# Graph kernel: 60 instead of 72 slotted source buckets in the last two layers, seven instead of five fetched row tiles, and later transposes

## The chip, the cores and the metric

The kernel runs on one core of one Trainium2 chip. The metric is the device time of one execution in microseconds; the time before is the median of three runs. The core's engines are named as in the profile: PE multiplies matrices (PEld is its loading of the stationary operand), DVE, ACT and POOL compute elementwise, SP and others issue DMAs. POOL also issues the indirect DMAs that fetch rows by a list of row numbers.

## The reference, cut to what matters

A graph of N = 12500 nodes with 128 float32 features and 200000 random directed edges passes four layers in a row. Each layer sums, for every node, the rows of its neighbours (plus edge information), and sends the sum through small dense products.

```python
def gnn0(h):                                   # layer 0, messages src -> dst, then a GRU cell
    msg = h[src] @ W_msg.T + b_msg + edge_embed[edge_type]
    messages = segment_sum(msg, dst, 12500)
    return gru_cell(messages, h)               # gates of 3 x 128

def gin(x, p, concat):                         # layers 1 to 3, with self loops added to the edges
    ee = ea @ enc_w + enc_b
    h = concatenate([x[ei[1]], ee], 1) if concat else x[ei[1]] + ee
    agg = segment_sum(h, ei[0], 12500)
    h = relu(batchnorm(agg @ w1 + b1))
    return h @ w2 + b2

x = layernorm(x + gnn0(x))
h = relu(gin(x, p0, False)); h = relu(gin(h, p1, True)); h = gin(h, p2, True)
out = layernorm(x + h)
```

## The kernel before

Nodes lie in NB = 98 blocks of 128. The edges are sorted on the chip, in a preparation of about 1180 us, by the block of the node that gets the sum (the target block, `o` in the code) and by the block of the node that is read (the source bucket, `b`). Every pair of target block and bucket has SL = 32 slots; four buckets make one tile of 128 slots. Features are held as three bf16 pieces side by side (H3 = 384 columns, 768 bytes a row), so that a product with a matrix of zeros and ones selects float32 rows.

One layer walks over the 98 target blocks. For a block it does the following:

- DVE builds two matrices of zeros and ones: `g` (L1546), which says which source row fills each slot, and `s` (`st` in the code, L1551, in four pieces), which says to which node of the block each slot is added.
- For each tile PE makes four gather matmuls of 32 columns (L1663), one for each bucket, from the source tables `X` in SBUF, tiles of seven buckets (XC = 7, 672 KB), into PSUM. Up to TG = 3 tiles form a group with three PSUM banks; the pool `psg` holds two groups.
- ACT, in layers 0 and 1 with DVE's help (L1669, L1670, L1672), copies the group to SBUF as `e` (the eviction; four buffers).
- PE adds the tiles of `e` to their nodes with one scatter matmul each (L1592, in `scatter`), into one accumulating PSUM bank `acc`, of which there is only one. `add_up_to(2)`, called after every second group, does the scatters of groups that were gathered two or more groups ago.
- After a block's last group `finish` adds the three pieces of `acc` to `s` (the float32 sums; L1614, L1617, L1618 on DVE), and, after every second block, appends a dense generator to `work`: `gru` in layer 0, `gin` in layers 1 to 3. A generator runs in pieces between its `yield`s; `tick` advances the oldest one by one piece. Two ticks, or three if more than one is waiting, follow each `add_up_to`. The dense pieces are transposes of the sums (L1464 in `gin`; L1412 and L1413 in `gru`), a copy of them on DVE (`sT`, L1466), the first products (L1473, L1474; in `gru` L1427 to L1429), the activations and gates on ACT (L1476), the second products (L1484), and what writes the result into the next layer's table.

Layers 0 and 1 have all 98 buckets in slots: 25 tiles, nine groups. Layers 2 and 3 have only IC = 72 buckets in slots, 18 tiles in six groups; the edges of the other buckets are listed for each target block, and their source rows are fetched one by one: `fetch` (L1568) is an indirect DMA on POOL's queue that brings 128 rows, 98 KB, from the table in HBM to a place of a ring. `rt` = 5 such row tiles stand for each target block (980 fetches in the two layers), and a matmul for each, with the same kind of one-hot columns, adds it to the same bank (L1597, in `scatter_row`). A block's groups 1 to 5 each ask for one fetch and scatter one row tile. The ring has 14 − 11 = 3 tiles of seven places, 21; 15 fetches are issued ahead of the loop. A fetch waits for its place: for the scatter matmul that read it last. `Slots.rows` prepares the row numbers and columns of the fetched tiles in layer 0, one window for each row tile.

POOL also fetches edge attributes (L719) in layers 0 and 1, paced by small copies called `token` (L1688); in layers 2 and 3 the ring's fetches are its work. In the layers only POOL's order is written by hand; a scheduler places PE's, DVE's and ACT's instructions. Before layers 1, 2 and 3 a loop over spilled edges (L663) brings all engines together, and the source tables of the new layer are loaded by SP and ACT queues.

Of the kernel before, what the change touches and what calls it, by code (L numbers as in the profile page):

```python
# [32 lines left out]
TG = 3  # L33
# [5 lines left out]
class Plan:  # L39
    def __init__(self, lst, ic, rt):  # L40
# [3 lines left out]
        self.row = self.kept = 0  # L44
        self.width = CELL + self.cells + (CELL + self.cells) % 2


IC = 72
CELL = 5
PLANS = (Plan("C", IC, 5),)  # L50
RT = sum(p.rt for p in PLANS)
TW = CELL + NTL
assert PLANS[0].rt <= CELL and CELL % 2 == NTL % 2 == 1
OV = 8
# [34 lines left out]
def gnn_kernel(ctx: ExitStack, tc: tile.TileContext, x, xx, src, dst, ea, et, w_msg, w_ihT, w_hhT, b_msg,  # L89
# [276 lines left out]
    XC = 7  # L366
# [834 lines left out]
    with by_hand(EN.Activation, EN.PE):  # L1201
# [34 lines left out]
        n = 0  # L1236
# [156 lines left out]
    def gru(i, b0, s):  # L1393
        q = b0 // 2
        if q % 2 == 0:
            four["xx"] = dq.tile([P, 2, 2, 2 * H], F32, name="xx")
            m = min(2, NB // 2 - q)
            nc.sync.dma_start(four["xx"][:, :m], xx[:, q:q + m])
        xb = four["xx"][:, q % 2, 0, :].rearrange("p (b f) -> p b f", b=2)
        xt = four["xx"][:, q % 2, 1, :]  # L1400
        yield
        c6 = dq.tile([P, 2, 6, NTX], BF16, name="c6")
        v = s[:, :, H:]
        times = lambda n: v[:, :, None, :].to_broadcast([P, 2, n, NTX])
        V.tensor_copy(c6[:, :, 0:3, :], times(3))
        V.tensor_sub(v, v, c6[:, :, 0, :])
        V.tensor_copy(c6[:, :, 3:5, :], times(2))
        V.tensor_sub(c6[:, :, 5, :], v, c6[:, :, 3, :])
        yield
        pt = psd.tile([P, 512], F32, name="d")  # L1410
        for k in range(2):
            T.transpose(pt[:, k * P:(k + 1) * P], s[:, k, 0:H], ident)  # L1412
            T.transpose(pt[:6 * NTX, 256:384].bitcast(BF16)[:, k * P:(k + 1) * P],  # L1413
                        c6[:, k, :, :].rearrange("p a b -> p (a b)"), identb)
        sT = dq.tile([P, 2 * P], F32, name="sT")
        V.tensor_copy(sT, pt[:, :256])
        cT = dq.tile([E6, 4 * P], BF16, name="cT")[:6 * NTX, :2 * P]
        A.copy(cT, pt[:6 * NTX, 256:384].bitcast(BF16))
        yield
        yield  # L1420
        yield
        gates = dq.tile([P, 2, 2 * H], F32, name="gates")
        n = dq.tile([P, 4, H], F32, name="n")[:, 0:2, :]
        for k in range(2):
            ks = slice(k * P, (k + 1) * P)
            pg = psd.tile([P, 512], F32, name="d")
            T.matmul(pg, cT[:, ks], w["ew"], start=True, stop=False, skip_group_check=True)  # L1427
            T.matmul(pg[:, 0:3 * H], sT[:, ks], w["wa"], start=False, stop=False, skip_group_check=True)
            T.matmul(pg[:, H:], xt[:, ks], w["whh"], start=False, stop=True, skip_group_check=True)  # L1429
            A.activation(gates[:, k, :], pg[:, H:3 * H], AF.Sigmoid)  # L1430
            V.tensor_mul(n[:, k, :], gates[:, k, 0:H], pg[:, 3 * H:])
            V.tensor_add(n[:, k, :], n[:, k, :], pg[:, 0:H])
            yield
            yield
            yield
        A.activation(n, n, AF.Tanh)
        yield
        y, k, whole = rows_of(b0)
        d = dq.tile([P, 2, H], F32, name="r3")
        V.tensor_sub(d, xb, n)  # L1440
        V.tensor_mul(d, d, gates[:, :, H:])
        V.tensor_add(n, n, xb)
        V.tensor_add(y[:, k:k + 2, :], n, d)
        if whole:
            yield from layernorm(y, *whole, False)

    def gin(i, b0, s):
        yield
        k4 = b0 % 4
        if k4 == 0:  # L1450
            m = min(4, NB - b0)
            while len(summed) < b0 + m:
                next(attr)
            four["eT"] = dq.tile([E6, 4 * P], BF16, name="cT")
            nc.sync.dma_start(four["eT"][:, :m * P], eaTd[:, b0 * P:(b0 + m) * P])
            if i == 3:
                four["xx"] = dq.tile([P, 2, 2, 2 * H], F32, name="xx")
                nc.sync.dma_start(four["xx"][:, 0].rearrange("p a (b f) -> p (a b) f", b=2)[:, :m, :], x1d[:, b0:b0 + m, :])
            else:
                four["o"] = dq.tile([P, 4, H], F32, name="n")  # L1460
        eT = four["eT"][:, k4 * P:(k4 + 2) * P]
        pt = psd.tile([P, 512], F32, name="d")
        for k in range(2):
            T.transpose(pt[:, k * P:(k + 1) * P], s[:, k, 0:H], ident)  # L1464
        sT = dq.tile([P, 2 * P], F32, name="sT")
        V.tensor_copy(sT, pt[:, :256])  # L1466
        yield
        yield
        ph = psd.tile([P, 2, 2 * P], F32, name="d")
        h1 = dq.tile([P, 2, 2 * P], F32, name="gates")  # L1470
        for m in range(2):
            ms = slice(m * P, (m + 1) * P)
            T.matmul(ph[:, m, :], w["w1"][:, ms], sT, start=True, stop=False)  # L1473
            T.matmul(ph[:, m, :], w[f"wc_{i - 1}"][:, ms], eT, start=False, stop=True)  # L1474
        for m in range(2):
            A.activation(h1[:, m, :], ph[:, m, :], AF.Relu, bias=w["shift"][:, i - 1, m:m + 1],  # L1476
                         scale=w["scale"][:, i - 1, m:m + 1])
        yield
        yield
        po = psd.tile([P, 512], F32, name="d")  # L1480
        for k in range(2):
            ks = slice(k * P, (k + 1) * P)
            for m in range(2):
                T.matmul(po[:, ks], h1[:, m, ks], w["w2"][:, m, :], start=(m == 0), stop=(m == 1))  # L1484
        bias = w["b2"][:, None, :].to_broadcast([P, 2, H])
        po3 = po[:, :256].rearrange("p (b f) -> p b f", b=2)
        if i < 3:
            o = four["o"][:, k4:k4 + 2, :]
            V.tensor_add(o, po3, bias)
            yield  # L1490
            V.tensor_scalar(o, o, 0.0, None, op0=OP.max)
            split3(o, i + 1, b0, b0 + 2 == NB)
            if k4 or b0 + 2 == NB:
                nc.sync.dma_start(by_node(ovf[i + 1], b0 - k4, k4 + 2), four["o"][:, :k4 + 2, :])
        else:
            y, k, whole = rows_of(b0)
            xb = four["xx"][:, 0].rearrange("p a (b f) -> p (a b) f", b=2)[:, k4:k4 + 2, :]
            V.tensor_add(xb, xb, bias)
            V.tensor_add(y[:, k:k + 2, :], po3, xb)
            if whole:  # L1500
                yield from layernorm(y, *whole, True)
# [1 line left out]

    token = ctile([1, 1], "token", BF16)
    LATE, BEHIND = 4, 8
    assert PLANS[0].rt == -(-PLANS[0].cells // TG) - 1

    def layer(i, rate):

# [2 lines left out]
        if i < 2:  # L1512
            nb, tiles, c0, tw, cell, row, rt = NB, NTL, a * (CELL - 1), TC, a, 0, 0
        else:
            nb, tiles, c0, tw, cell, row, rt = p.ic, p.cells, 0, p.width, CELL, p.row, p.rt
        xf = -(-nb // XC)
        rb = NB // XC - xf
        wid = H3 + (NTX if cells_only else 0)
        groups = -(-tiles // TG)
        work = []  # L1520
        due = -8 if cells_only else 0
        stack = ExitStack()
# [6 lines left out]
        def slots_of(o):  # L1529

            n = nb * SL
            inr = rp.tile([P, 2 * IC * SL], BF16, name="inr")[:, :per * n]
            inr = inr.rearrange("p (b c) -> p b c", c=n)
# [38 lines left out]
        def tick():  # L1572
            if work and next(work[0], "end") == "end":
                work.pop(0)

        ready = []
        row_slots = slots.rows() if cells_only else None
        for _ in range(rb * rt):
            fetch()
        for _ in one_hots(0):  # L1580
            pass
# [1 line left out]
        picked = []  # L1583
# [8 lines left out]
                T.matmul(sums[o][:, :wid], st[:m, :, cell + t], e[:m, j, :wid], start=(t == 0),  # L1592
                         stop=(t == tiles - 1), skip_group_check=True)

        def scatter_row(o, st, j):
            if 0 <= j < rt:
                T.matmul(sums[o][:, :H3], st[:, :, row + j], place(o * rt + j), start=False, stop=False,  # L1597
                         skip_group_check=True)

# [35 lines left out]
            yield from dense  # L1635

        def add_up_to(n):
            while len(picked) > n:
                o, st, e, k = picked.pop(0)
                if k == groups - 1:  # L1640
                    scatter_row(o, st, k - 1)
                scatter(o, st, e, k)
                if k < groups - 1:
                    scatter_row(o, st, k - 1)
                if k == groups - 1:
                    finish(o)

        for o in range(NB):
            g, st = ready.pop(0)
# [5 lines left out]
            for k in range(groups):  # L1655
                n = min(TG, tiles - TG * k)
# [18 lines left out]
                    V.tensor_tensor(e[:m, :n, H3:], iota[:m, None, :NTX].to_broadcast([m, n, NTX]),  # L1675
                                    typecol[:m, o, t:t + n, None].to_broadcast([m, n, NTX]), op=OP.is_equal)
                picked.append((o, st, e, k))
                if k:
                    fetch()
                next(pieces, None)  # L1680
                if cells_only:
# [8 lines left out]
                    due -= 1  # L1690
                if (o * groups + k) % 2 == 0:
                    continue
                add_up_to(2)
                for _ in range(2 + (len(work) > 1)):
                    tick()
            for _ in pieces:
                pass
# [63 lines left out]
```

## Time and profile before

| what | value |
|---|---|
| three runs | 6322.02 us median, 6303.31 to 6328.62 |
| the profiled execution | 6326.88 us, of which the span holds 6325.1 us |
| mean granted TensorE clock | 0.884 of full speed |
| busy: PE, PEld | 4936.9 us (78%), 3045.2 us (48%) |
| busy: DVE, ACT, POOL | 3758.4 (59%), 3696.8 (58%), 3318.8 us (52%) |
| first and last gathers: layer 0, layer 1 | 1184 to 2914 us, 2915 to 4364 us |
| first and last gathers: layer 2, layer 3 | 4366 to 5338 us, 5340 to 6310 us |
| fetches of rows (L1568) | 980, 959.9 us on POOL, mean 979 ns |

The times of the layers overlap a little with what follows them: the dense work of a layer's last blocks runs while the next one begins. The page's slices of the span show this course; each digit is the share of a fortieth of the span, 158 us, in tenths:

```profile
## 2 busy tenths in 40 slices
PE   3881421378888888887888888887999998899998
PEld 3871121144444444443555454444666665566666
DVE  9976788666666666665555555553444443444444
```

The first seven slices are the preparation, the next twenty layers 0 and 1, the last thirteen layers 2 and 3. Rows of groups are read so: line, engine, operation, result and source with their shapes, the number of instructions; then busy time and the mean of one in ns; then how long the engine was idle ahead of them, and which instruction ended how much of it. In a time line a row is start, duration, engine and line, and in brackets the idle time before it with what ended it.

### The profile page before, as it was taken

To read this page: it belongs to the slowest core of one execution; us is meant where nothing else is said; L and a number is where in the kernel's file an instruction comes from. 1 tells how busy PE (TensorE), PEld (TensorE's weight loads), DVE (VectorE), ACT (ScalarE), POOL (GpSimd) and SP (SyncE) were. 2 spreads that over 40 slices of the span, in tenths; PEclk is the share of its full clock that TensorE was granted. 3 is DMA by queue.
4 is the path that set the end of the run, shared out by engine and by line. 5 is a ranking of instruction groups with operands and counts; after the bars stand their busy time and mean duration, and the time that the engine had idled before them with its cause. 6 is when DMAs were issued, how large, how long until landed. Compare 5 with 4: busy or idle time off the path is not lost. (4 is left out here: it accounts for less than half of the span.)

```text
span 6325.1 us, 129827 instructions
## 1 busy us (share of the span) xinstructions
PE 4936.9 (78%) x50669; PEld 3045.2 (48%) x50669; DVE 3758.4 (59%) x9291; ACT 3696.8 (58%) x5320; POOL 3318.8 (52%) x4247
## 2 busy tenths in 40 slices
PE   3881421378888888887888888887999998899998
PEld 3871121144444444443555454444666665566666
DVE  9976788666666666665555555553444443444444
ACT  7770211155555555554666666665777776677776
POOL 1004677366566565655666666652555553555553
PEclk9755555589999899998999999998999999999999
DMA  1001300122222222223222222223444445344443
GB/s 70 21 1 32 100 18 7 42 72 82 73 82 75 76 84 84 76 75 136 82 81 78 80 81 75 78 80 135 138 139 138 147 140 167 123 143 137 137 145 105
DMA packets 278298, 575.36 MB, mean 91 GB/s; under 512 B 74332, under 2 KB 170216, under 8 KB 277026
## 3 DMA queue, kind: packets, MB, share of 16 engines
q1 hardware_dynamic: 159138, 416.84, 19.3%
q0 software_dynamic: 105920, 116.17, 7.6%
q10 hardware_dynamic: 12616, 33.99, 1.6%
q8 instruction: 397, 6.50, 0.4%
q14 instruction: 227, 1.86, 0.1%
HBM read 478.02 MB, written 88.73 MB: 90 GB/s over the span
## 5 line engine op out<-in xcount | busy, mean ns | idle before, releaser
L1672 ACT CAST e<-g 128x1152 bf16<-128x1152 f32 (+1 forms) x2156 | 2239.6, 1063 | 844.0 <-PE g L1663 510.5
L1663 PE MATMUL g<-x,g 128*32 128x384 bf16 x33320 | 1880.7, 338 | 442.0 <-ACT e L1672 195.0
L719 POOL DMA_INDIRECT eat<-in_ea,eidcol x1666 | 1813.6, 1089 | 545.8 <-issue 416.0
L1592 PE MATMUL acc<-e,s 128*128 128x384 bf16 (+3 forms) x8428 | 1913.3, 349 | 82.3 <-DVE s L1618 53.7
L1592 PEld LDWEIGHTS <-s 128*128 128x128 bf16 (+1 forms) x8428 | 1132.0, 152 | 733.7 <-issue 515.0
L1568 POOL DMA_INDIRECT x<-table,rowcol x980 | 959.9, 979 | 955.1 <-PE acc L1597 645.2
L1663 PEld LDWEIGHTS <-g 128*32 128x32 bf16 x33320 | 807.9, 97 | 1287.2 <-issue 986.6
L1669 ACT CAST e<-g 128x768 bf16<-128x768 f32 x784 | 627.4, 800 | 574.5 <-PE g L1663 236.6
L1551 DVE TENSOR_TENSOR s<-iotas,outcol 128x832 bf16<-128x832 bf16 (+1 forms) x1568 | 875.0, 567 | 95.8 <-PE acc L1592 52.1
L1670 DVE CAST e<-g 128x384 bf16<-128x384 f32 x784 | 435.2, 555 | 576.1 <-ACT e L1669 479.0
L1688 POOL COPY token<-e 1x1 bf16<-1x1 bf16 x1412 | 344.4, 244 | 814.8 <-ACT e L1669 456.5
L1546 DVE TENSOR_SCALAR g<-inr,pidx 128x3136 bf16<-128x3136 bf16 (+1 forms) x392 | 365.0, 931 | 462.2 <-PE g L1663 439.7
L557 PE MATMUL acc<-ot,oa 125*98 125x101 bf16 x1600 | 295.9, 359 | 125.9 <-ACT ot L538 85.7
L557 PEld LDWEIGHTS <-oa 125*98 125x98 bf16 x1600 | 292.0, 277 | 129.0 <-issue 82.0
L1614 DVE TENSOR_TENSOR s<-s,acc 128x128 f32<-128x128 f32 x376 | 107.1, 285 | 414.7 <-PE acc L1592 315.5
L538 ACT ACTIVATE ot<-dbb,bias 125x160 bf16<-125x160 bf16 (+2 forms) x1078 | 332.3, 408 | 16.6 <-PE acc L557 15.9
L1597 PE MATMUL acc<-x,s 128*128 128x384 bf16 x980 | 288.5, 327 | 9.7 <-DMA x<-table,rowcol 9.7
L802 POOL IOTA num<- 98x2176 uint16 x1 | 1.9, 1946 | 459.3 <-DMA sortedB<-keyB 459.3
L1476 ACT ACTIVATE gates<-d,shift,scale 128x256 f32<-128x256 f32 x294 | 149.7, 559 | 158.6 <-PE d L1474 146.9
L752 PEld LDWEIGHTS <-eoh 128*128 128x128 bf16 x1666 | 116.7, 162 | 237.6 <-DVE eoh L746 183.3
L1675 DVE TENSOR_TENSOR e<-iota,typecol 128x30 bf16<-128x30 f32 (+1 forms) x882 | 152.9, 180 | 123.9 <-PE acc L1592 41.8
L1473 PE MATMUL d<-sT,wset 128*128 128x256 f32 x588 | 184.1, 406 | 49.3 <-DVE sT L1466 44.0
(426 smaller groups left out, 4736.5 us busy)
## 6 DMA issues: line engine op xcount, KB each, us to landing
inr<-inrow SPq DMA_DIRECT2D x196, 784.0 KB
inr<-inrow SPq DMA_DIRECT2D x98, 1152.0 KB
table<-x SPq DMA_DIRECT2D x72, 384.0 KB
eat<-in_ea,eidcol POOLq DMA_INDIRECT x1666
s<-ovf SPq DMA_DIRECT2D x69, 256.0 KB
x<-table,rowcol POOLq DMA_INDIRECT x980
x<-table ACTq DMA_DIRECT2D x19, 672.0 KB
xx<-in_xx SPq DMA_DIRECT2D x24, 512.0 KB
```

The source lines that it names most:

```text
L538: A.activation(self.ot[j % 2][:, b, :ENDS[j] - c0], dbb[:, c0:ENDS[j]], AF.Sign, bias=self.bias[:, b:b + 1], scale=-1.0)
L557: T.matmul(cps[:NB, :NB + NQ - 1], self.oa[c // HC][:, :, c % HC], self.ot[j % 2][:, :, c - (ENDS[j - 1] if j else 0)], start=(c == 0), st ...
L719: G.indirect_dma_start(out=at[:, t, :], out_offset=None, in_=ea, in_offset=bass.IndirectOffsetOnAxis(ap=eidcol[:, b, t:t + 1], axis=0))
L1546: V.tensor_scalar(g[:, :nb * SL], inr[:, o % per, :nb * SL], pidx, None, op0=OP.is_equal)
L1551: V.tensor_tensor(st[:, f0:f0 + P // 4, :], iotas[:, f0:f0 + P // 4, :tw], outcol[a][:, o, None, c0:c0 + tw].to_broadcast([P, P // 4, tw]) ...
L1568: G.indirect_dma_start(out=place(asked), out_offset=None, in_=tables[i], in_offset=bass.IndirectOffsetOnAxis(ap=rowcol[:, o, p.kept + j:p. ...
L1592: T.matmul(sums[o][:, :wid], st[:m, :, cell + t], e[:m, j, :wid], start=(t == 0), stop=(t == tiles - 1), skip_group_check=True)
L1663: T.matmul(pg[c * SL:(c + 1) * SL, j, :H3], g[:, b * SL:(b + 1) * SL], piece(X, b), start=True, stop=True)
L1669: A.copy(e[:, :2, :H3], pg[:, :2, :H3])
L1670: V.tensor_copy(e[:, 2, :H3], pg[:, 2, :H3])
L1672: A.copy(e[:m, :n, :H3], pg[:m, :n, :H3])
L1688: G.tensor_copy(token, e[0:1, 0, 0:1])
```

## The change

Four things are changed together.

The split in layers 2 and 3 is another: 60 buckets in slots instead of 72, so 15 tiles in five groups instead of 18 in six, and `rt` = 7 fetched row tiles for each target block instead of 5 (1372 fetches instead of 980). With it the source tables shrink from 11 to 9 tiles, the ring grows to 14 − 9 = 5 tiles of seven, 35 places, and 28 instead of 15 fetches are issued ahead of the loop. `g` has 1920 columns instead of 2304, and `s` 22 for each node instead of 24. `Slots.rows` does seven windows instead of five.

Row tiles are spread over all groups: `of_group(k)` gives groups 0 to 4 of a block 1, 1, 2, 1 and 2 fetches and scatters, where before each group but the first had one.

`gru` and `gin` have one empty piece more, ahead of the transposes.

`add_up_to` does one tick between `finish` of a block and the scatters of the next one, where the same call does both, and this tick is taken off those that follow.

```diff
-IC = 72
-CELL = 5
-PLANS = (Plan("C", IC, 5),)
+IC = 60
+CELL = 7
+PLANS = (Plan("C", IC, 7),)
@@ gru, behind the pieces c6 and ahead of the transposes
         yield
+        yield
         pt = psd.tile([P, 512], F32, name="d")
@@ gin, behind the loads and ahead of the transposes
+        yield
         eT = four["eT"][:, k4 * P:(k4 + 2) * P]
@@ layer
-    assert PLANS[0].rt == -(-PLANS[0].cells // TG) - 1
...
+        of_group = lambda k: range(rt * k // groups, rt * (k + 1) // groups)
...
-        for _ in range(rb * rt):
+        for _ in range((rb * XC - rt) // rt * rt if rt else 0):
             fetch()
...
-        def scatter_row(o, st, j):
-            if 0 <= j < rt:
+        def scatter_rows(o, st, k):
+            for j in of_group(k):
                 T.matmul(sums[o][:, :H3], st[:, :, row + j], place(o * rt + j), start=False, stop=False,
                          skip_group_check=True)
...
         def add_up_to(n):
+            early = 0
             while len(picked) > n:
                 o, st, e, k = picked.pop(0)
                 if k == groups - 1:
-                    scatter_row(o, st, k - 1)
+                    scatter_rows(o, st, k)
                 scatter(o, st, e, k)
                 if k < groups - 1:
-                    scatter_row(o, st, k - 1)
+                    scatter_rows(o, st, k)
                 if k == groups - 1:
                     finish(o)
+                    if len(picked) > n:
+                        tick()
+                        early = 1
+            return early
...
-                if k:
+                for _ in of_group(k):
                     fetch()
...
-                add_up_to(2)
-                for _ in range(2 + (len(work) > 1)):
+                for _ in range(2 + (len(work) > 1) - add_up_to(2)):
                     tick()
```

## The prediction

> **What bounds the kernel now.** I first cut the span into stretches and read each engine's busy time and the granted clock there: layer 1 with side fetches on POOL, layer 1's last blocks without them, the steady parts of layers 2 and 3, and the stall after layer 3's start.
>
> ```profile
> core 0: us, PE busy (x) PEld busy (x) DVE busy (x) ACT busy (x) POOL busy (x), PEclk, DMA share, GB/s
> 3000.00:4250.00 1250.00, 1077.55 (x11946) 626.00 (x11946) 681.58 (x1535) 776.03 (x1031) 807.18 (x1247) 0.96 0.26 79
> 4275.00:4350.00 75.00, 69.61 (x806) 40.94 (x802) 42.33 (x91) 52.10 (x71) 10.38 (x43) 1.00 0.26 87
> 4450.00:5300.00 850.00, 796.22 (x9168) 523.79 (x9161) 392.70 (x940) 646.51 (x715) 429.54 (x444) 1.00 0.44 141
> 5400.00:6250.00 850.00, 795.79 (x9212) 527.29 (x9211) 414.92 (x1180) 624.80 (x642) 443.40 (x448) 1.00 0.44 139
> 5373.00:5394.00 21.00, 3.68 (x20) 1.45 (x20) 0.00 (x0) 1.07 (x2) 12.92 (x14) 0.60 0.24 69
> ```
>
> In the steady parts PE is busy 796.2 of 850 us (93.7%): PE sets the pace there, ACT has 24% to spare, POOL half. The last row is the opposite: POOL works, everybody else stands. Then the groups of the steady part of layer 2, with how long each engine idled ahead of them and for whom:
>
> ```profile
> L1672 ACT CAST e<-g 128x1152 bf16<-128x1152 f32 x533 | 579.2, 1122 | 157.4 <-PE g L1663 111.4 <-PE d L1464 20.9 <-PE acc L1597 17.4
> L1568 POOL DMA_INDIRECT x<-table,rowcol x444 | 429.7, 968 | 420.5 <-PE acc L1597 315.6 <-issue 45.1 <-PE acc L1592 38.6
> L1592 PE MATMUL acc<-e,s 128*128 128x384 bf16 x1597 | 346.5, 335 | 18.3 <-DVE s L1618 15.4 <-DVE r L1353 2.9
> L1663 PE MATMUL g<-x,g 128*32 128x384 bf16 x6408 | 328.6, 328 | 24.6 <-ACT e L1672 19.4 <-issue 0.9
> L1473 PE MATMUL d<-sT,wset 128*128 128x256 f32 x180 | 54.9, 398 | 9.3 <-DVE sT L1466 8.8 <-issue 0.3
> L1614 DVE TENSOR_TENSOR s<-s,acc 128x128 f32<-128x128 f32 x89 | 25.6, 288 | 206.5 <-PE acc L1592 147.1 <-PE acc L1597 59.4
> ```
>
> 89 blocks (L1614 x89) in 850 us: 9.55 us a block, 8.95 of it PE busy and 0.60 idle. POOL waits mostly for PE to free a ring place (L1597): the ring is kept full. Last, time lines of a stretch where POOL is not held back, the start of layer 3: POOL's, ACT's and PE's lines.
>
> ```profile
> 5387.68 0.95 POOL L1568 DMA_INDIRECT x<-table,rowcol  x1 [0.30 <-issue]
> 5388.93 0.95 POOL L1568 DMA_INDIRECT x<-table,rowcol  x1 [0.30 <-issue]
> 5394.16 1.23 POOL L1568 DMA_INDIRECT x<-table,rowcol  x1 [4.28 <-remote]
> 5393.03 2.14 ACT L1672 CAST e<-g 128x1152 bf16<-128x1152 f32 x2 [19.93 <-remote]
> 5394.20 2.17 PE L1663 MATMUL g<-x,g 128*32 128x384 bf16 x24 [17.12 <-ACT e L1672]
> ```
>
> 24 fetches run from 5359.99 to 5389.88, one each 1.25 us (0.95 and 0.30 of issue). PE's finished groups reach nobody: ACT stands 19.93 us, and it, POOL and PE go on only after the last fetch. Layer 2's start has the same, 27 fetches from 4382.9 to 4416.7 and PE idle 15.17 us. So a POOL stream of some ten fetches or more holds back PE's signals. DVE is idle in it (0.00 of 21 us).
>
> The Trainium skill, page "SBUF — State Buffer", section "Who interferes with whom", says that only the port pair of DVE and GpSimd contends, and that PE and ACT never wait on anyone. By it the longer stream below would cost PE nothing and the sum would be 35 us lower; the rows above differ from it, and I go by the rows.
>
> **The change, part by part.** The profiled execution took 6326.9 us (span 6325.1 and 1.8 around it); the runs' median is 6322.0, 4.9 lower.
>
> Steady blocks of layers 2 and 3. Their loop starts some 2 blocks after the layer does, so 96 each, 192 in all. 18 tiles become 15. In PE's time line of 4800 to 4824 a three-tile group runs 24 gather matmuls at 0.04 us (0.96) and 0.13 to switch, and a scatter step comes each 0.163 us. Three tiles fewer: 3 × (0.16 + 0.163) = 0.97 us off. Two fetched rows' scatters more: 2 × 0.163 = 0.33 on. PE busy falls from 8.95 to 8.31 us a block. ACT loses one 1.12 us eviction, DVE shorter one-hots; both were beside PE and count nothing.
>
> POOL: 7 fetches a block instead of 5, 7 × 1.25 to 1.27 (0.968 mean and 0.30) = 8.75 to 8.89 us. That was 6.3 and hidden below 9.55; now it lies above PE's 8.31. So 8.8 us a block is the floor.
>
> PE's idle 0.60: the late transposes and the tick between finish and the next scatter put dense work where PE waited for DVE (L1473 8.8, L1592 15.4, together 24.2 of 850 us, 0.27 a block). I take 0.27 off, leaving 0.33. Against it, a POOL that hardly rests sends PE's signals late. No row shows 14 fetches per two blocks; the nearest is layer 1, where POOL is busy 807 of 1250 us and PE idles 13.8%, against 7.2% in layer 1's last blocks with POOL nearly idle. The 6.6 points (other work differs too) are 0.6 us of a block. Then 8.31 + 0.33 + 0.6 = 9.24, 0.31 less than now, × 192 = −60 us. Bounds: the floor 8.8 (−144); at the top a gap after each stream. In layer 0 a stream of some ten fetches was followed by PE gaps of 2 to 4 us (one of 3.32 at 2475); 3 us per block pair on 8.6 makes 10.1, +106. I take the middle, since streams are one or two fetches long now, and the ring lets them grow only as far as PE lags.
>
> Layer starts. The prefetch goes from 15 to 28 and the ring from 21 to 35 places. The streams were 24 and 27, three to six more than the 21 places; 35 places make about 38 and 41: 14 more × 1.25 = 17.5 us each, 35 for both. Bounds: 0, if the extra rows are all won back later from a POOL that is behind, and 50.
>
> Gather tables: 9 instead of 11 tiles of 672 KB are loaded at each start; at the 420 GB/s read there, 1344 KB take 3.2 us: −6 for both, or 0 if the stall covers it.
>
> Layers 0 and 1. The empty pieces put transposes and the products behind them a group pair later. Up to that much PE idles there: in layer 1, 3000 to 4250 us:
>
> ```profile
> L1473 PE MATMUL d<-sT,wset 128*128 128x256 f32 x176 | 58.3, 425 | 29.5 <-DVE sT L1466 27.1 <-issue 0.9 <-DVE e L1670 0.8
> L1464 PE MATMUL d<-ident,s 128*128 128x128 f32 x88 | 28.9, 333 | 20.5 <-DVE s L1618 8.6 <-issue 7.4 <-remote 2.6
> ```
>
> 50 us, and in layer 0 about 26 (L1427 for ACT's cT 18.9, L1412 and L1413 7.3). A third of the 76 is assumed to come back at another wait, for the evictions that the same groups wait for: −50. All of it could (0), or dense work could end later still (+20); at best −95, with the two layers' scaled to their full length. Two more windows of fetched rows in layer 0 (window fetches x5 now): POOL 2 × 1.27, DVE about 2 × 1.3, little on PE: +5 at most, taken whole. Together −45.
>
> Sum: 6326.9 − 60 + 35 − 6 − 45 = 6251; less a part of the 4.9 by which the median lies lower, I say 6250.
>
> **Rivals.** (a) POOL becomes the bound and all else hides under it: 8.8 a block. For it: PE's work of 8.31 leaves half a microsecond for late signals. Against: the rows of layer 1, with PE idle 13.8%. 6327 − 144 + 35 − 6 − 45 = 6167. 15%.
>
> (b) Slower: POOL, behind by a few places, streams ten and more fetches each block pair, and after each PE stands for its late signals, as in layer 0; 10.1 us a block. Place: the PE waits of L1663 for L1672 in layers 2 and 3. It decides as soon as a block passes 9.63 us, where 192 × 0.08 = 16 and the starts' 35 eat up the 51 of the other terms. For it: 8.75 to 8.89 of POOL against 8.31 of PE, so POOL is the slower of the two and its streams have no natural end. Against: a lagging PE asks for fewer fetches. 6327 + 106 + 35 − 6 − 45 = 6417. 33%.
>
> (c) Waits refill: the block stays at 9.45, the early layers give back 20 only: 6327 − 19 + 35 − 6 − 20 = 6317. 17%.
>
> (d) The change doesn't do what it says: only if list C of leftover edges filled; counted from the inputs it is empty before and after (at most 892 of 896 rows a block). Under 1%, left out.
>
> **How the numbers follow.** My forecast has 35%. 0.5% is about what a measurement of this kernel can tell from none: below 6290 faster, above 6354 slower. Forecast and (a) are faster, (c) the same, (b) slower: 0.50, 0.17, 0.33. The range takes in nearly all of the forecast, (c), (a)'s upper half and (b) up to its price less 20 us: 6155 to 6400. The forecast's own range, with block 9.0 to 9.4 and the early layers 0 to −70, is 6190 to 6310.
>
> **What would show it.** Steady windows: PE busy near 8.3 us a block, POOL at 72 to 77% busy, and L1568 waiting for issue, no longer for L1597. If L1663 waits for L1672 over 60 us in 850, (b) is at work. First gathers of layers 2 and 3 to their first full block 17 us later than now. In layer 1 the waits of L1464 and L1473 under 20 us in all. I am wrong above all if PE's signals in a stream of four to eight fetches are later than layer 1 suggests, or if the streams break off by themselves.

## The result and the profile after

The changed kernel takes 6646.32 us (median of four runs, 6618.45 to 6652.16) against 6324.95 us before: 1.05 times as long, with an interval of 1.0477 to 1.0523. It is slower, on the side of rival (b), and by more than that rival's price. The profiled execution has a span of 6647.4 us, 322.3 more than before.

From first to last gather in the two traces, layers 0 and 1 together take 3169.9 us instead of 3177.8 (8 less), layer 2 (from 4363 us before, not 4366) 1132.0 instead of 974.5, layer 3 1141.6 instead of 969.5. In each of the last two, the first four blocks take about 98 us instead of 76.4 and 78.3 (41 more for both). The blocks behind them make up all the rest, about 288 us: from block 8 to block 97, counted from 0, one takes 10.96 and 11.08 us instead of 9.56 and 9.51.

In the changed kernel the lines named before are L1570 (fetch), L1594 (scatter), L1599 (rows' scatter), L1620 (last add of `finish`), L1670 (gather), L1679 (eviction), L1466 and L1475 (transpose, first product). The same view of stretches, for layer 1 and the steady parts of layers 2 and 3:

```profile
core 0: us, PE busy (x) PEld busy (x) DVE busy (x) ACT busy (x) POOL busy (x), PEclk, DMA share, GB/s
3000.00:4250.00 1250.00, 1083.73 (x12151) 638.06 (x12149) 684.32 (x1552) 788.50 (x1049) 837.53 (x1272) 0.96 0.27 81
4500.00:5350.00 850.00, 692.93 (x6913) 428.08 (x6911) 308.08 (x806) 481.45 (x539) 527.13 (x537) 0.93 0.44 131
5650.00:6500.00 850.00, 685.17 (x6789) 421.18 (x6791) 334.23 (x1012) 449.66 (x462) 523.71 (x528) 0.92 0.42 126
```

Now no engine is busy all the time: PE 82% and 81%, POOL 62%, ACT 57% and 53%. The granted clock, 1.00 before, is 0.93 and 0.92. The groups of the steady part of layer 2:

```profile
L1570 POOL DMA_INDIRECT x<-table,rowcol x537 | 527.9, 983 | 325.0 <-PE acc L1599 100.4 <-issue 83.8 <-PE g L1670 75.7
L1679 ACT CAST e<-g 128x1152 bf16<-128x1152 f32 x383 | 424.3, 1120 | 341.3 <-PE g L1670 142.9 <-PE acc L1599 72.4 <-remote 47.5
L1594 PE MATMUL acc<-e,s 128*128 128x384 bf16 x1149 | 288.7, 364 | 71.0 <-DVE s L1620 56.3 <-DVE s L1553 5.4 <-DVE s L1619 3.7
L1670 PE MATMUL g<-x,g 128*32 128x384 bf16 x4608 | 263.4, 337 | 82.8 <-ACT e L1679 44.3 <-issue 37.6
L1616 DVE TENSOR_TENSOR s<-s,acc 128x128 f32<-128x128 f32 x77 | 21.9, 285 | 151.6 <-PE g L1670 105.0 <-PE acc L1594 39.8 <-PE d L1486 6.8
```

77 blocks in 850 us are 11.04 us each: PE busy 9.00, idle 2.04. PE waits for ACT's evictions and DVE's adds, while ACT (341 us) and DVE stand idle for PE: they wait in a circle. One scatter takes 364 ns, 335 before, with the same shape, which fits the lower clock (335 / 0.93 = 360). So PE's work shrank, and what is left of it runs slower and with more than three times the idle time. The Trainium skill ("TensorE: Matmul & The Clock Gate", "HAM oscillation — how this bites in real kernels") says that waits of more than about 3.4 us between bursts of matmuls let the clock fall back. These rows agree that idle time lowers it, with 1.00 at 6% idle and 0.92 to 0.93 at 19%, but not with that bound: in the steady part of layer 2 no wait of PE was longer than 3.1 us.

The start of layer 3, POOL's time line, of a stream of 42 fetches that began at 5506.8:

```profile
5556.91 0.95 POOL L1570 DMA_INDIRECT x<-table,rowcol  x1 [0.30 <-issue]
5558.16 0.95 POOL L1570 DMA_INDIRECT x<-table,rowcol  x1 [0.30 <-issue]
5566.00 1.22 POOL L1570 DMA_INDIRECT x<-table,rowcol  x1 [6.90 <-remote]
```

and PE's, in the stream and behind it:

```profile
5542.35 0.83 PE L1670 MATMUL g<-x,g 128*32 128x384 bf16 x7 [12.59 <-issue]
5557.26 0.48 PE L1670 MATMUL g<-x,g 128*32 128x384 bf16 x1 [2.32 <-issue]
5566.95 1.15 PE L1670 MATMUL g<-x,g 128*32 128x384 bf16 x12 [9.21 <-ACT e L1679]
```

as before, only longer.

### The profile page after: what moved, and what is told of

It is laid out like the page before. It is cut to its first block, busy times and chain, and to the rows that moved or that the text cites. A ratio compares the mean times of both kernels' runs of the same rounds, so it can differ in the third digit from the quotient of the medians.

```text
span 6647.4 us, 125163 instructions
## 1 busy us (share of the span) xinstructions
PE 4939.8 (74%) x48125; PEld 2988.3 (45%) x48125; DVE 3684.1 (55%) x9311; ACT 3498.7 (53%) x5128; POOL 3722.7 (56%) x4641
## 5 line engine op out<-in xcount | busy, mean ns | idle before, releaser
L1679 ACT CAST e<-g 128x1152 bf16<-128x1152 f32 (+1 forms) x1960 | 2044.1, 1056 | 1397.0 <-PE g L1670 619.7
L1670 PE MATMUL g<-x,g 128*32 128x384 bf16 x30968 | 1843.4, 343 | 699.3 <-ACT e L1679 332.4
L719 POOL DMA_INDIRECT eat<-in_ea,eidcol x1666 | 1790.4, 1075 | 536.1 <-issue 394.0
L1594 PE MATMUL acc<-e,s 128*128 128x384 bf16 (+3 forms) x7840 | 1882.2, 361 | 220.8 <-DVE s L1620 136.0
L1570 POOL DMA_INDIRECT x<-table,rowcol x1372 | 1352.6, 986 | 890.4 <-issue 253.2
L1670 PEld LDWEIGHTS <-g 128*32 128x32 bf16 x30968 | 776.3, 98 | 1547.0 <-issue 1272.6
L1594 PEld LDWEIGHTS <-s 128*128 128x128 bf16 (+1 forms) x7840 | 1039.5, 151 | 915.7 <-issue 539.2
L1553 DVE TENSOR_TENSOR s<-iotas,outcol 128x832 bf16<-128x832 bf16 (+1 forms) x1568 | 841.2, 553 | 642.7 <-PE acc L1594 252.1
L1695 POOL COPY token<-e 1x1 bf16<-1x1 bf16 x1412 | 376.9, 267 | 801.5 <-ACT e L1676 417.1
L1599 PE MATMUL acc<-x,s 128*128 128x384 bf16 x1372 | 407.0, 355 | 15.7 <-DMA x<-table,rowcol 13.9
L1599 PEld LDWEIGHTS <-s 128*128 128x128 bf16 x1372 | 194.9, 149 | 87.9 <-issue 68.6
```

Source lines behind the costliest of these rows:

```text
L719: G.indirect_dma_start(out=at[:, t, :], out_offset=None, in_=ea, in_offset=bass.IndirectOffsetOnAxis(ap=eidcol[:, b, t:t + 1], axis=0))
L1553: V.tensor_tensor(st[:, f0:f0 + P // 4, :], iotas[:, f0:f0 + P // 4, :tw], outcol[a][:, o, None, c0:c0 + tw].to_broadcast([P, P // 4, tw]) ...
L1570: G.indirect_dma_start(out=place(asked), out_offset=None, in_=tables[i], in_offset=bass.IndirectOffsetOnAxis(ap=rowcol[:, o, p.kept + j:p. ...
L1670: T.matmul(pg[c * SL:(c + 1) * SL, j, :H3], g[:, b * SL:(b + 1) * SL], piece(X, b), start=True, stop=True)
L1679: A.copy(e[:m, :n, :H3], pg[:m, :n, :H3])
L1695: G.tensor_copy(token, e[0:1, 0, 0:1])
```

## The experiments

Theory 1: while POOL issues indirect DMAs, PE's signals reach the other engines late; at 14 fetches in two blocks POOL hardly rests, so that PE, ACT and DVE wait for each other, and PE's clock falls. Theory 2: the new order (empty pieces, the tick inside `add_up_to`, the spread rows) makes PE wait for DVE and ACT.

The runs were made in five groups, each on one chip with the kernel before beside it. This table gives for each the ratio to before on that chip and, from its trace, a block of layers 2 and 3 (8 to 97) and the sum of the first four blocks of both. Numbers are us.

| run | chip: before | median | ratio, interval | block L2, L3 | starts L2 + L3 |
|---|---|---|---|---|---|
| before | the result's | 6324.95 | 1 | 9.56, 9.51 | 76 + 78 |
| changed | the result's | 6646.32 | 1.05, 1.0477 to 1.0523 | 10.96, 11.08 | 98 + 98 |
| a_five | chip 3: 5960 | 5786.91 | 0.971, 0.969 to 0.9729 | 8.30, 8.36 | 50 + 51 |
| a_plain | chip 3 | 5948.28 | 0.9983, 0.9971 to 0.9994 | 9.00, 9.11 | 47 + 48 |
| b_order | chip 3 | 5893.73 | 0.9894, 0.9877 to 0.991 | 9.08, 8.92 | 52 + 53 |
| b_seven | chip 3 | 5982.83 | 1.0036, 1.0021 to 1.0052 | 9.17, 9.33 | 49 + 53 |
| after_again | chip 0: 6326 | 6661.91 | 1.0522, 1.0485 to 1.0559 | 11.16, 10.93 | 98 + 98 |
| before_again | chip 0 | 6329.85 | 1.0008, 0.999 to 1.0026 | 9.54, 9.52 | 77 + 80 |
| a_five_2 | chip 0: 6322 | 6388.2 | 1.0103, 1.0066 to 1.0141 | 9.62, 9.72 | 88 + 94 |
| b_seven_2 | chip 0 | 6745.04 | 1.0667, 1.0624 to 1.0711 | 11.94, 11.85 | 79 + 84 |
| b_order_2 | chip 0 | 6282.9 | 0.994, 0.9917 to 0.9964 | 9.46, 9.26 | 77 + 80 |
| b_order_ring7 | chip 0 | 6638.08 | 1.0493, 1.0462 to 1.0524 | 11.33, 11.50 | 65 + 68 |
| b_order_short | chip 4: 6327 | 6256.34 | 0.9873, 0.9844 to 0.9903 | 9.48, 9.28 | 58 + 61 |
| b_pool | chip 4 | 6283.11 | 0.9934, 0.9903 to 0.9965 | 9.43, 9.43 | 60 + 66 |
| a_plain_2 | chip 7: 6387 | 6829.82 | 1.069, 1.0647 to 1.0732 | 11.79, 11.59 | 97 + 99 |
| a_short | chip 7 | 6669.3 | 1.0438, 1.0399 to 1.0478 | 11.21, 11.26 | 65 + 68 |

**Fewer fetches in the changed kernel, the order alone on either side, more fetches in the kernel before.** The first group.

a_five issues only five of a block's seven fetches:

```diff
             o, j = divmod(asked, rt)
+            if asked >= rb * XC and j >= 5:
+                asked += 1
+                return
```

> The changed kernel, but in the loop only the first five of a block's seven fetches are issued (the scatters of the other two read what the ring holds, so the sums of layers 2 and 3 lack those rows' values). PE's instructions are those of the changed kernel. Theory 1 (POOL's dense fetches make PE's signals late, and PE's gaps lower its clock): a block falls from 11.0 to 8.4 to 9.0 us, PEclk back to 0.98 or more, run near 6200. Theory 2 (the new order of transposes, ticks and rows makes PE wait for DVE and ACT): a block stays above 10.3 us, run above 6500.

a_plain takes the empty pieces and the early tick out of the changed kernel:

```diff
@@ gru and gin
-        yield
@@ add_up_to
-                    if len(picked) > n:
-                        tick()
-                        early = 1
```

> The changed kernel without the empty pieces in gru and gin and without the tick inside add_up_to; split and spread stay. Theory 1: blocks of layers 2 and 3 stay at 10.7 to 11.5 us, run 6600 to 6700. Theory 2: blocks fall towards 9.3 us and the run below 6450.

b_order puts them into the kernel before (72 buckets, five rows):

> The kernel before (72 buckets, five rows) with only the empty pieces and the tick inside add_up_to. Theory 1: layers 2 and 3 within 0.3 us of 9.55 a block; layers 0 and 1 about 10 us shorter as in the changed kernel; run 6270 to 6320. Theory 2: blocks of layers 2 and 3 above 10.3 us, run above 6450.

b_seven adds two fetches a block to the kernel before:

```diff
-            n %= rb * XC
+            n %= (rb - 1) * XC
...
-        for _ in range(rb * rt):
+        for _ in range((rb - 1) * rt):
...
                 if k:
                     fetch()
+                if rt and k in (2, 4) and asked < NB * rt:
+                    G.indirect_dma_start(out=ring[2][:, extra % XC, :], out_offset=None, in_=tables[i],
+                                         in_offset=bass.IndirectOffsetOnAxis(ap=rowcol[:, o, p.kept + k // 3:p.kept + k // 3 + 1], axis=0))
+                    extra += 1
```

> The kernel before with two more fetches a block (into the seven places of the ring's third tile, which nothing reads; the ring is cut to 14 places). PE, ACT and DVE have the work of before. Theory 1: a block goes from 9.55 to 11 us or more, PEclk falls below 0.95, run above 6550. Theory 2: a block stays below 9.8 us, run near 6350.

These runs fell on a chip where the kernel before itself takes 5960 us, 365 less than in the result. The expectations were priced for the other kind and missed: a_five and b_order came out lower, a_plain did not lose at all, b_seven cost 0.4% and not 3.5%. Their traces say why. In b_order's the start of layer 3 has 76 fetches with no pause of half a microsecond, and nobody stands for the length of it; POOL, then PE, then ACT, in the middle of that stream:

```profile
5019.66 0.95 POOL L1570 DMA_INDIRECT x<-table,rowcol  x1 [0.30 <-issue]
5020.91 0.95 POOL L1570 DMA_INDIRECT x<-table,rowcol  x1 [0.30 <-issue]
5018.51 1.16 PE L1670 MATMUL g<-x,g 128*32 128x384 bf16 x24
5021.05 1.16 PE L1670 MATMUL g<-x,g 128*32 128x384 bf16 x24
5019.29 2.14 ACT L1679 CAST e<-g 128x1152 bf16<-128x1152 f32 x2 [0.41 <-PE g L1670]
5021.83 2.14 ACT L1679 CAST e<-g 128x1152 bf16<-128x1152 f32 x2 [0.24 <-PE g L1670]
```

A group's eviction follows its gathers at once, with POOL in the same stream that stopped everything in the runs of before. The Trainium skill ("SBUF — State Buffer", "Who interferes with whom") says that on SBUF's ports only DVE and GpSimd contend, and that PE and ACT wait on nobody. On this chip neither is held up while POOL fetches; on the others they are (17.12 and 19.93 us at the start of layer 3). The page speaks of ports, and no run here shows that ports are the cause. In a_plain's trace POOL never rests: one stream of 686 fetches fills layer 2.

```profile
4150.00:5000.00 850.00, 768.83 (x8480) 516.31 (x8476) 385.05 (x987) 575.44 (x662) 649.02 (x660) 1.00 0.55 160
```

660 fetches in 850 us are 1.288 us each, seven of them 9.02 us, and a block takes 9.00: this is rival (a), POOL as the bound. PE is busy 768.83 us, 8.14 for each block of 9.00, at full clock: so much is the work of the new split.

**The two kernels again.** Both unchanged, to see the chips apart from the kernels.

> The changed kernel, unchanged, on whatever chip this falls on. In the runs of before and after, PE's signals came late while POOL fetched, and the change cost 5%; on the chip of the four runs so far they came at once and before took 5960 us. Theory 1 (late signals make the loss): where signals come at once POOL's pace of 7 x 1.29 us sets a block, 9.0 us, and the run is within 1% of before, 5900 to 5980; where they are late again, 6600 to 6680 against 6320. Theory 2 (order): 4 to 6% slower on either.

> The kernel before, unchanged, for a trace on the chip of the same call. Theory 1: where signals come at once, a block of layers 2 and 3 takes 9.1 to 9.2 us, no engine stands at the layers' starts, 5960; where they are late, 9.55 us and 6320. Theory 2 says nothing of it.

On chip 0 the signals are late again, and the loss is there again: 1.0522, blocks of 11.16 and 10.93 us, PE's clock 0.91 to 0.92. Between the chips the kernel before differs by 6% (5960 and 6326). What makes one chip differ from the others is not known.

**The same on the chip with late signals.** The third group repeats a_five, b_seven and b_order there, and tries a short ring.

> The changed kernel with five of seven fetches issued in the loop, again (layers 2 and 3 lack the two rows' values), wanted on a chip where PE's signals come late (before at 6320). There theory 1: a block at 8.6 to 9.3 us against 11.0, run 6150 to 6330, below before or near it; theory 2: a block above 10.3 us, run above 6500. Where before is at 5960: 5790 as measured.

> The kernel before with two more fetches a block that nothing reads, again. Where signals are late, theory 1: a block at 10.5 to 11.5 us against 9.55, PEclk below 0.97, run above 6500; theory 2: below 9.8 us, run near 6340. Where before is at 5960: 5983 as measured.

> The kernel before with the empty pieces and the tick inside add_up_to alone, again. Where signals are late, theory 1: blocks of layers 2 and 3 at 9.2 to 9.6 us, layers 0 and 1 some 10 us shorter, run 6270 to 6330; theory 2: a block above 10.3 us, run above 6450. Where before is at 5960: 5894 as measured.

> The same with the ring cut to seven places and five fetches ahead of the loop, so that a layer starts with some eight fetches in a row and not 24 to 27. Theory 1, where signals are late: no stall over 6 us at the starts, 20 to 30 us less for each of layers 2 and 3 than the kernel with the order alone, run 6210 to 6290; theory 2: no difference. Where before is at 5960: within 10 us of 5894, since nothing stalls at the starts there; above it if seven places are too few to hide the fetches.

The two fetches alone are worth 1.0103 against 1.0522: a block of the changed kernel falls from 11 to 9.62 and 9.72 us with all its order kept. Put into the kernel before, two fetches that nobody reads cost 2.4 us a block (more than was written down) and 6.7%, though their 2 × 1.27 us on POOL and the 6.3 of the other five fit into the 9.55 of a block; on chip 3 the same edit cost 0.4%. Theory 2 falls: the order alone is 0.6% faster. But theory 1 priced a_five_2 too low (6150 to 6330, measured 6388): with five fetches a block the changed kernel still is 0.1 to 0.2 us slower than before, though PE has less to do. Its fetches come two at a time in one group, and in rows of 2.6 on average where those of the kernel before come in rows of 1.7 (pauses under 0.5 us); whether that is the reason was not tried.

That the handovers are late in the steady blocks too can be read from the traces. Where ACT stood idle ahead of an eviction, the time from the end of the group's last gather to the eviction's start was 0.11 us on chip 3 (median of b_seven and of a_five, and still 0.11 for nine in ten). In layers 2 and 3 it was 0.55 and 0.37 us in the kernel before, 1.27 and 1.18 in the changed kernel and 1.19 and 1.05 in b_seven_2; one in ten took over 1.3, 3.0 and 2.6 us there. The ends of matmuls are modelled in the profile, so this doesn't tell a late signal from a product that itself comes late.

b_order_ring7 has the ring cut to one tile of seven places, and five fetches ahead:

```diff
-            n %= rb * XC
+            n %= XC
...
-        for _ in range(rb * rt):
+        for _ in range(rt):
```

It says nothing on the theories: with five fetches ahead, a fetch stands in the program before the scatter that should have read its place, so that this scatter waits for the later fetch and adds other rows than it should. A block took 11.4 us, and from 4500 to 5250 us PE waited 71.8 us for fetched rows.

**A short start, and POOL busy with something else.** b_order_short is b_order_ring7 with three fetches ahead instead of five, which restores the order of reads and fetches. b_pool replaces b_seven's two fetches by memsets.

```diff
-                    G.indirect_dma_start(out=ring[2][:, extra % XC, :], ...
+                    G.memset(ring[2][:, 0:3, :], 0.0)
```

> The kernel before with the empty pieces and the tick inside add_up_to, a ring of seven places and three fetches ahead of the loop (with five, a fetch overtook the scatter of its place; with three it doesn't), so that a layer starts with some eight fetches in a row. Theory 1, where PE's signals are late (before at 6320): no stall over 6 us at the starts of layers 2 and 3, 20 to 30 us less for each than with the order alone (6283), 6220 to 6260. Where before is at 5960: within 15 us of 5894.

> The kernel before with the ring cut to 14 places and two memsets of 128x1152 on POOL a block where the other kernel had two more fetches (POOL as busy, but without DMAs). If any work on POOL makes PE's signals late, a block goes to 11 us or more, run above 6550 where before is at 6320. If it is the issue of indirect DMAs alone, a block stays at 9.4 to 9.8 us, run 6290 to 6370; where before is at 5960, near 5965 either way.

The stretch 4500 to 5250 us of b_seven_2, of b_pool, and then POOL's two groups in b_pool there:

```profile
4500.00:5250.00 750.00, 601.50 (x6355) 378.46 (x6354) 270.50 (x645) 449.29 (x495) 425.85 (x434) 0.94 0.41 127
```

```profile
4500.00:5250.00 750.00, 711.58 (x8198) 468.56 (x8196) 395.06 (x836) 578.09 (x637) 558.50 (x558) 1.00 0.47 144
```

```profile
L1569 POOL DMA_INDIRECT x<-table,rowcol x399 | 388.9, 975 | 191.7 <-PE acc L1598 123.1 <-issue 50.8 <-PE g L1664 15.1
L1682 POOL MEMSET x<- 128x1152 bf16 x159 | 170.9, 1075 | 0.1
```

With memsets of 1075 ns POOL is busier (558.5 of 750 us, against 425.9) than with fetches of 974 to 988 ns, and PE is busy 95% at full clock, against 80% at 0.94. An idle ACT begins its evictions as in the kernel before (medians of 0.9 and 0.4 us in layers 2 and 3, nine in ten within 1.4). So it is the indirect DMAs, not a busy POOL, that make the handovers late. Whether their issue on POOL or their transfers do it is not shown, since the memsets take away both. (The two ran on different chips, both with before at 6322 to 6327.)

b_order_short starts layers 2 and 3 with 12 and 8 fetches in a row instead of 27 and 24; PE waits at most 3.6 us there for an eviction, and the starts take 58 + 61 us instead of 77 + 80. At 6256 us it met what was written down. It is the fastest of the kernels tried where signals are late, 0.9873 of before, and keeps 72 buckets and five rows.

**How the loss divides.** The last group.

> The changed kernel without the empty pieces and the tick inside add_up_to, again, wanted where PE's signals are late. Theory 1 with the order as a small gain: a block at 11.0 to 11.5 us, run 6640 to 6750. If the order's new places cost time under late signals: a block at 10.2 to 10.8, run 6480 to 6600. Where before is at 5960: 5948 as measured.

a_short gives the changed kernel a ring of 14 places and seven fetches ahead:

```diff
-            n %= rb * XC
+            n %= 2 * XC
...
-        for _ in range((rb * XC - rt) // rt * rt if rt else 0):
+        for _ in range(rt):
```

> The changed kernel with a ring of 14 places (not 35) and seven fetches ahead of the loop (not 28). Theory 1, where signals are late: the starts of layers 2 and 3 lose their long streams and 25 to 40 us each, steady blocks stay at 10.8 to 11.2, run 6570 to 6610. If the long ring is what lets POOL stream, steady blocks fall below 10.5 and the run below 6540. Where before is at 5960: 5900 to 5960.

On this chip (before 6387) the changed kernel itself was not run; against its 1.0500 and 1.0522 elsewhere, the short start is 0.6 to 0.8 points better, with starts of 65 + 68 us instead of 98 + 98, and no help in the steady blocks (11.21 and 11.26 us): the ring's length is not what lets POOL stream. Without the empty pieces and the tick it is 1.069: inside the changed kernel too the order seems to take time off, 1.7 to 1.9 points, more than the 0.6 that it is worth in the kernel before. Both comparisons set ratios of different chips beside each other and are no firmer than that. Both medians lie above what was written down, by 59 and 80 us, on a chip where before is 60 us higher.

## Why the prediction was wrong

**What bounds the kernel** was read rightly, and so was the mechanism: PE's signals are late while POOL fetches, and the starts are the place to see it. Rival (b) named one of the waits where it would show (L1663 for L1672; now 44.3 and 68.6 us in 850, on either side of its 60). In layer 2 most of PE's 157 us of idle time are elsewhere: 56.3 us of scatters waiting for DVE's adds, 37.6 us of "issue" ahead of gathers.

**The steady blocks: the term for PE's idle time failed.** The step was "The 6.6 points (other work differs too) are 0.6 us of a block", with "I take the middle". Term by term, per block:

| term | predicted | measured |
|---|---|---|
| PE busy | 8.31, at full clock | 9.00, at 0.93 (8.14 at full clock in a_plain, chip 3) |
| PE idle | 0.33 + 0.6 = 0.93 | 2.04 |
| block | 9.24 | 11.04 |

Of the 1.80 us that were missing, 1.11 are idle time and 0.69 longer busy time. Layer 1 was the wrong row. It has about seven fetches a block, but spread over nine groups and 14.4 us, with copies on POOL between them that wait for ACT and so break the streams. Closest was a row of the same stage: the layers' starts, where dense fetches stopped PE entirely. The argument that streams break off since "the ring lets them grow only as far as PE lags" held only in part: streams in the steady blocks are three fetches long on average and nine at most, and the handovers are late all the same. The clock was a term left out, though the stall's row showed 0.60 beside 1.00. As an estimate, 8.31 us at a clock of 0.93 are 8.9, most of the 0.69; but busy time does not grow by the clock alone, since b_seven_2 has 9.6 us a block at 0.95 where the same work took 8.95 at 1.00. Rival (b)'s 10.1 had the same two faults and was a microsecond short. (The 24 gather matmuls of the working are two groups of three tiles, not one; its 0.16 us a tile is right.)

**POOL's floor** of 8.75 to 8.89 was 0.1 to 0.4 too low on a chip with prompt signals: 9.00 and 9.11 us, at 1.288 us a fetch.

**The starts** were right: streams of 38 and 41 and 35 us predicted, 42 and 42 fetches and 41 us measured. With the short ring of a_short they take 65 + 68 us, on another chip.

**Layers 0 and 1** were wrong: −45 predicted, −8 measured in these traces and +10 on chip 0 (3190.6 against 3180.9 us), where b_seven_2, which leaves these layers as they were, took 3162.2. So no gain is clear of the spread. The waits that were named did go, but others grew. Layer 1, 3000 to 4250 us, the scatters and gathers before, then after:

```profile
L1592 PE MATMUL acc<-e,s 128*128 128x384 bf16 (+1 forms) x2150 | 486.3, 351 | 0.8 <-DVE s L1618 0.8
L1663 PE MATMUL g<-x,g 128*32 128x384 bf16 x8428 | 484.4, 335 | 113.9 <-DVE e L1670 61.2 <-ACT e L1672 41.7 <-issue 6.9
```

```profile
L1475 PE MATMUL d<-sT,wset 128*128 128x256 f32 x176 | 52.3, 392 | 1.4 <-DVE own L757 1.3
L1466 PE MATMUL d<-ident,s 128*128 128x128 f32 x88 | 25.8, 303 | 1.3 <-issue 0.9 <-DVE own L757 0.2 <-ACT ownT L779 0.2
L1594 PE MATMUL acc<-e,s 128*128 128x384 bf16 x2193 | 494.9, 352 | 20.3 <-DVE s L1620 13.6 <-issue 3.4 <-DVE s L1553 2.0
L1670 PE MATMUL g<-x,g 128*32 128x384 bf16 x8589 | 494.0, 335 | 139.3 <-DVE e L1677 73.6 <-ACT e L1679 52.0 <-issue 5.3
```

The idle time ahead of L1475 and L1466 fell from 50.0 to 2.7 us, but that ahead of the scatters rose from 0.8 to 20.3 and ahead of the gathers from 113.9 to 139.3: 45 of 47 returned, in a stretch in which 1.9% more gathers ran. From first to last gather layer 1 is 23.5 us shorter (1423.5 and 1447.0), less than the two thirds that the prediction kept, and layer 0, where a gain was forecast too, 15.6 longer (1745.3 and 1729.7). Why layer 0 lost is open. On chip 3, without late signals, the same order shortened the two layers by 29 us (a_five against a_plain: 2902.6 and 2931.5) and by 44 (b_order against b_seven: 2896.1 and 2940.5), where the forecast for the order was 50; in layer 1 alone by 39 and 37.

**The tables** (−6) were not seen apart from the starts.

**The range** ended at 6400, some 20 us short even of rival (b), and its top rested on one gap per block pair, where the trace has several short ones. The chances of 33% for (b) and 50% for faster weighed a longer block against PE's smaller work, and took the first too lightly. The best case for the early layers, −95, is −88 by the rows that it scales.

## What to carry to other kernels

Before work is moved from an engine at its limit to POOL's indirect DMAs, look in the trace for a place where they run in a row and see whether other engines' waits end late there. If they do, price the move by that place, with every handover between engines delayed and PE's clock lowered, and not by POOL's free time. Taking a wait away ahead of one instruction gains only what the next wait on the same engine doesn't take back: name that next wait first. Measure on more than one chip when the price hangs on a delay of signals: the new split with the old order (a_plain) took 6.9% more time than before on one chip and no more on another.

## What the runs showed of the hardware that was not expected

One kernel took 5960 us on one chip and 6322 to 6387 on three others. b_order shows where: on chip 0 it had the same clock of 1.00 in the blocks of layers 2 and 3 and the same 0.95 us for a fetch in a row as on chip 3, but took 118 us more in these two layers and 269 more in layers 0 and 1. In layers 2 and 3 the difference goes with POOL's indirect DMAs: on chip 3 a stream of 686 fetches, 884 us long, lets an eviction begin 0.11 us behind its gathers (median of a_plain), on the others one of 24 stops ACT for 20 us. Memsets of about the same length on POOL delay nobody there either (b_pool). Whether it is the same in layers 0 and 1, where POOL fetches edge attributes, was not tried. In the stream of 42 fetches PE did single matmuls 2.8 us apart, each behind 2.32 us of "issue" wait, so that PE's own sequencing, too, seems to be held; that was not followed further.

The traces record the granted clock in stretches of 3.41 us, each at 1 or at 0.5. From 4500 to 5340 us of the changed kernel, 29 stretches at 1 were followed by one at 0.5; PE was busy for 9 to 54% of them, without a wait over 3.1 us, and for 46% or more of those followed by another at 1. In b_seven_2 (22 stretches) the two sides are 9 to 46% and 49% or more; in the kernel before, at 59% or more, the clock did not fall there. So here about half a stretch of idle time was enough, in several short waits.
